# A two-layer graph attention kernel: fewer rows of a node summed on TensorE in layer 1, and another order of loads at the seam between the layers

## The chip, the cores and the metric

The kernel runs on one core of one Trainium2 chip. The metric is the device time of one execution in microseconds (us). Before the change, three timed executions took 5579.89, 5581.57 and 5582.52 us; the median, 5581.57 us, is the time before. A further execution was recorded by the hardware profiler and took 5586.68 us.

The engines are named as the profile names them: PE is TensorE (PEld its weight loads), DVE is VectorE, ACT is ScalarE, POOL is GpSimd, and SP is the engine from whose queue most plain DMAs are issued. Each engine works through its own instructions in program order and waits on semaphores for the others.

## What is computed

The reference is a graph attention network of two layers with residual paths, on 10,000 nodes of 768 features and 170,000 edges (self loops included; the layers add one more self loop to each node). Cut to what matters:

```python
def gat_conv(x, edge_index, W, a_src, a_dst, bias, heads, out_ch, concat):
    ei = _add_self_loops(edge_index, n)
    src, dst = (ei[0], ei[1])
    xl = (x @ W).reshape(n, heads, out_ch)
    alpha_src = einsum('nhc,hc->nh', xl, a_src)
    alpha_dst = einsum('nhc,hc->nh', xl, a_dst)
    e = leaky_relu(alpha_src[src] + alpha_dst[dst], 0.2)
    e = exp(e - segment_max(e, dst)[dst])
    alpha = e / (segment_sum(e, dst)[dst] + 1e-16)
    out = segment_sum(xl[src] * alpha[:, :, None], dst)
    ...
h = relu(layer_norm(gat_conv(x, ..., W1, ..., 4, 256, True), g1, be1)) + (x @ Wr1 + br1)
h = layer_norm(gat_conv(h, ..., W2, ..., 1, 768, False), g2, be2) + (h @ Wr2 + br2)
x = layernorm(x + h)
```

Layer 1 has 4 heads of 256 columns (1024 together), layer 2 one head of 768. Everything is 32-bit floating point.

## The kernel before, in words

**Blocks.** Nodes are sorted by their number of incoming edges and cut into 79 blocks of 128, one node to a partition. A block t has SLOTS[t] slots: slot k holds, for each of the 128 nodes, the table row of its k-th neighbour. The program fixes the number of slots of each block in advance, 8 to 41, 1377 in all. The blocks are taken in an order in which the slots rise to 41 in the middle (block 39) and fall again. Below, n is the number of slots of a block. "Row" means one slot: one gathered row for each of 128 nodes. 

**Three stages.** Stage 0 multiplies x by W1 and writes table 1; beside it `prepare()` sorts the nodes on the other engines, and `weight_steps()` loads W2, adds two columns to it, loads Wr1, and computes the product of br1 with W2, whose results are the tile `lift` and the DRAM row `shift`. Then `ordered_layer1()` and `ordered_layer2()` run one after the other. (`general_path()` is for inputs that do not fit; it does not run here.)

**A block of layer 1.** POOL gathers rows of table 1 into a ring of 28 slots (`Ring.fetch`, L413), each with one indirect DMA of 128 rows. A slot is fetched again when its row was used. When all rows of the block are there, `logits` (L458 to L466) and `normalised` compute the attention weights e. The weighted sum is then split:

- the first m rows, m = `on_pe(t)`, are summed on PE: for each row and head ACT makes a diagonal matrix of the weights (L691) and PE multiplies it with the row into PSUM (L697). The rows 0 and 1 come first, then the rest in a second batch;
- of the other rows, `weigh` adds to the same PSUM tile on DVE. Counted from m, every fourth row is multiplied and added on DVE (four instructions at L496, one for each head); the three behind it are multiplied on ACT (L485, four instructions) and added on DVE with one instruction (L492).

The sums of block t+1 are prepared inside block t: `logits` is issued when block t has three rows left, the diagonals and PE sums behind it, if the two blocks fit into the ring. The statistics of the finished block (`deviation`, L538 to L542) and its normalisation (`scaled`, L551 to L554) follow on DVE. On ACT, the square root of the statistics (L542) stands between the two batches of diagonals. Behind the second batch stands `store(t - 2)`: ACT copies the finished row of an earlier block (L716), POOL scatters it into table 2 (L718), and behind that stand POOL's next gathers. PE further does transposes (L560), x times Wr1 (`product(xT, wr1, ...)`) and h times W2 (`product(hT, w2, ...)`), both at L166. `to_layer2` stores h for the second layer (L767, on SP's queue).

**The seam.** `ordered_layer2` gathers from table 2 into a ring of 38 slots. It loads Wr2 into the place of W2 (the tile w2), so this load follows the last product of layer 1; six pieces of the tile wr1 serve as buffers for h, x and a work tile. ACT's queue issues the loads of b2, g2, be2, br2, br1 and, behind an addition on DVE, `shift`. DVE adds br2 to be2 (L817), spreads br1 (L576), adds `shift` to b2 (L821), and only then comes to the logits of block 0.

**A block of layer 2.** PE computes x + h times Wr2 in PSUM (`residual`, L862 and L865); columns 0 to 511 of the attention sum are made on DVE (L496), columns 512 to 767 on PE with diagonals (L846, L851) into the residual's PSUM tile. `residual(t + 1)` is issued at the head of block t. In front of block 0 stands `residual(0)`, then the product of br1 with Wr2, then `residual(1)`, and only then the PE sums of block 0. A ring slot is free when both DVE and PE have used its row.

Of the kernel before, what the change touches and what calls it, by code (L numbers as in the profile page):

```python
# [34 lines left out]
P = 128  # L35
# [13 lines left out]
DIAGONALS = 5  # L49
ON_PE2 = 512  # L50
SHARE = 4
ON_PE1 = 5


def chunk_counts(n_edges):
# [23 lines left out]
def gnn_kernel(ctx, tc, x, x_cols, src, dst, src_col, dst_col, W1, a_src1, a_dst1, b1, g1, be1, Wr1, br1,  # L79
# [50 lines left out]
    loops = consts.tile([P, NT], F32, name="loops")  # L130
    fits = consts.tile([1, 1], I32, name="fits")
    lift = consts.tile([P, 1], F32, name="lift")

    def spread(pool, v, name):

        n = v.shape[-1] if len(v.shape) == 1 else v.shape[0] * v.shape[1]
        b = pool.tile([P, n], F32, name=name)
        nc.scalar.dma_start(b, bass.AP(tensor=v.tensor, offset=v.offset, ap=[[0, P], [1, n]]))
        return b

    def weights(pool, w, name, more=0):
# [17 lines left out]
    def product(aT, w, n, pool=None):  # L159

        k = w.shape[1]
        p = (pool or ps_big).tile([P, 2 * BANK], F32, name="big")
        for c in range(0, n, BANK):
            e = min(n, c + BANK)
            for j in range(k):
                nc.tensor.matmul(p[:, c:e], aT[:, j, :], w[:, j, c:e], start=(j == 0), stop=(j == k - 1))  # L166
        return p
# [399 lines left out]
    def load(s, w):  # L567
        nc.sync.dma_start(s[:, :, :w.shape[1]], w.rearrange("(k p) n -> p k n", p=P))

    def spread_br1(pool, name):  # L570

        b = pool.tile([P, K1], F32, name="br1_c")
        with nc.allow_non_contiguous_dma(reason="1024 numbers"):
            nc.scalar.dma_start(b, br1.rearrange("(k p) -> p k", p=P))
        to = pool.tile([P, K1, P], F32, name=name)
        nc.vector.tensor_copy(to, b[:, :, None].to_broadcast([P, K1, P]))  # L576
        return to

    wp = ctx.enter_context(tc.tile_pool(name="wp", bufs=1, side="right"))
# [2 lines left out]
    with tc.tile_pool(name="w1", bufs=1) as w1p, tc.tile_pool(name="l1", bufs=2) as io, \  # L582
            psum_for_products(), tc.manual_schedule():
        w1 = w1p.tile([P, K0, C1], F32, name="w1")
        xTs = {}

        def load_x(t):
            if t < NT:
                xTs[t] = io.tile([P, K0, P], F32, name="xT", bufs=3)
                nc.sync.dma_start(xTs[t], x_cols[t])  # L590

        load_x(0)
        for k in range(K0):
            nc.sync.dma_start(w1[:, k, :], W1[k * P:(k + 1) * P, :])
        load_x(1)
        as_b, ad_b = spread(w1p, a_src1, "as1_b"), spread(w1p, a_dst1, "ad1_b")
        none = w1p.tile([P, R1], F32, name="none")[:1]
        nc.vector.memset(none[:, :C1], 0.0)
        nc.vector.memset(none[:, C1:], -BIG)
        nc.scalar.dma_start(table1[NP:NP + 1, :], none)  # L600
        nc.scalar.dma_start(table2[NP:NP + 1, :], none[:, C1 - C2:C1 + 2 * H2])


        b1_b = w1p.tile([P, R1], F32, name="none")[:, :C1]
        nc.scalar.dma_start(b1_b, bass.AP(tensor=b1.tensor, offset=b1.offset, ap=[[0, P], [1, C1]]))

        def weight_steps():

            brT = spread_br1(w1p, "brT")
            yield
            yield
            load(w2, W2)
            for i, a in enumerate((a_src2, a_dst2)):
                vec = spread(w1p, a, "a2")
                for k in range(K1):
                    yield
                    m = io.tile([P, C1], F32, name="scr")[:, :C2]
                    nc.vector.tensor_mul(m, w2[:, k, :C2], vec)  # L620
                    nc.scalar.activation(m, m, AF.Copy, accum_out=w2[:, k, C2 + i:C2 + i + 1])
            load(wr1, Wr1)
            yield
            q = product(brT, w2, R2)
            row = io.tile([P, R1], F32, name="row")
            nc.scalar.copy(row[:, :R2], q[:, :R2])
            nc.vector.tensor_add(lift, row[:, C2:C2 + 1], row[:, C2 + 1:R2])
            nc.scalar.dma_start(shift, row[0:1, :C2])


        steps = itertools.zip_longest(prepare(), weight_steps())
        for t in range(NT):
            p = product(xTs.pop(t), w1, C1)
            row = io.tile([P, R1], F32, name="row")
            nc.scalar.copy(row[:, :C1], p[:, :C1])  # L635
            for i, vec in enumerate((as_b, ad_b)):
                m = io.tile([P, C1], F32, name="scr")
                nc.vector.tensor_mul(m, p[:, :C1], vec)  # L638
                for h in range(H1):
                    s = slice(h * DH1, (h + 1) * DH1)  # L640
                    nc.scalar.activation(m[:, s], m[:, s], AF.Copy,
                                         accum_out=row[:, C1 + i * H1 + h:C1 + i * H1 + h + 1])
            nc.gpsimd.tensor_add(row[:, :C1], row[:, :C1], b1_b)  # L643
            load_x(t + 2)
            nc.sync.dma_start(table1[t * P:(t + 1) * P, :], row)
            next(steps, None)
        for _ in steps:
            pass
# [7 lines left out]
    def ordered_layer1():  # L656
        nonlocal ps_big
        with tc.tile_pool(name="b1", bufs=1) as pool, tc.tile_pool(name="small1", bufs=2) as small, \
# [15 lines left out]
            def on_pe(t):  # L674


                return min(max((2 * SLOTS[t] - 15) // 5, 1), ON_PE1, SLOTS[t])

            def weights_of(t):

# [123 lines left out]
    def ordered_layer2():  # L804
        nonlocal ps_big
        with tc.tile_pool(name="b2", bufs=1) as pool, tc.tile_pool(name="small2", bufs=2) as small, \
                tc.tile_pool(name="ps_acc2", bufs=2, space=PSUM) as ps_acc, \
                tc.tile_pool(name="ps_q2", bufs=3, space=PSUM) as ps_big, tc.manual_schedule():
            ring = Ring(pool, table2, R2, RING2)
            ring.fetch(SLOTS[0])  # L810

            wr2, parts = w2[:, :, :C2], [wr1[:, k, :] for k in range(K0)]
            load(wr2, Wr2)
            b2_b, g2_b, be2_b = (spread(pool, v, n) for v, n in ((b2, "b2"), (g2, "g2"), (be2, "be2")))
            more = pool.tile([P, C2], F32, name="out")
            nc.scalar.dma_start(more, bass.AP(tensor=br2.tensor, offset=br2.offset, ap=[[0, P], [1, C2]]))
            nc.vector.tensor_add(be2_b, be2_b, more)  # L817
            brT = spread_br1(pool, "brT")
            more = pool.tile([P, C2], F32, name="out")
            nc.scalar.dma_start(more, shift.to_broadcast([P, C2]))  # L820
            nc.vector.tensor_add(b2_b, b2_b, more)  # L821

            def fetch_x(t):

# [64 lines left out]
            ins = {t: fetch_x(t) for t in range(min(2, NT))}  # L889
            ring.fetch(RING2)  # L890
            rs = {0: residual(0)}
            q = product(brT, wr2, C2)
            last = iter(())
            ready = []
            assert whole(0) and NT > 1
            for t in range(NT):
                n = SLOTS[t]
                if t + 1 < NT:
                    rs[t + 1] = residual(t + 1)
                h = parts[4 + t % 2][:, :C2]  # L900
                if not whole(t):
                    for _ in last:
                        pass
                    ad = small.tile([P, H2], F32, name="ad")
                    nc.vector.tensor_add(ad, ring.slot(FIRST[t])[:, C2 + H2:], lift)
                    attend_parts(small, ring, h, h, ad, b2_b, H2, DH2, t)
                    last = norms(t, h, rs[t], [h])
                else:
                    e = (ready or list(weights_of(t)))[0]
                    acc = ps_acc.tile([P, BANK], F32, name="acc")  # L910
                    next(last, None)
                    ready, ahead, turn = [], iter(()), n
                    if t + 1 < NT and SLOTS[t + 1] + LEAD <= ring.size:

                        ahead = weights_of(t + 1)
                        turn = min(max(n // 3, n + SLOTS[t + 1] + 2 * LEAD - ring.size), n - LEAD)
                    for k in range(n):
                        if k in (turn, turn + LEAD):
                            ready += itertools.islice(ahead, 1)
                        if k in (LEAD, 2 * LEAD, 3 * LEAD):  # L920
                            next(last, None)
                        weigh(acc, ring.slot(FIRST[t] + k), e[:, k], ON_PE2, None if k else b2_b)
                        ring.fetch(FIRST[t] + k + 1 + ring.size)
                        if t + 2 < NT and k == n // 2:
                            ins[t + 2] = fetch_x(t + 2)
                    ready += ahead
                    for _ in last:
                        pass
                    if not t:
                        nc.vector.tensor_add(be2_b, be2_b, q[:, :C2])  # L930
                    last = norms(t, h, rs[t], [acc, rs[t][:, C2:2 * C2 - ON_PE2]])
                if t + 2 < NT and t + 2 not in ins:
                    ins[t + 2] = fetch_x(t + 2)
# [272 lines left out]
```

## Time and profile before

| What | Before |
|---|---|
| profiled execution | 5586.68 us |
| its span, first to last instruction | 5584.8 us |
| PE busy | 4822.9 us (86%) |
| DVE busy | 4279.6 us (77%) |
| POOL busy | 3367.2 us (60%) |
| ACT busy | 3140.8 us (56%) |
| mean load of the DMA engines | 283 GB/s |
| granted TensorE clock, mean | 0.939 |
| stage 0 | 0 to 892 us (first gather of layer 1) |
| layer 1 | 892 to 3540 us (first gather of layer 2) |
| layer 2 | 3540 us to the end |

Read the busy shares stage by stage. In layer 1 (892 to 3540 us) PE is busy for 2285 of 2648 us, DVE for 2179, ACT for 2045, POOL for 1455. In layer 2 PE is busy for 1682 of 2045 us, DVE for 1616, POOL for 1490, ACT for 740. POOL's busy time is the time of its DMA instructions; between two of them lie about 0.30 us of issue that is not counted as busy.

The period of a block of layer 1, taken from one store of h (L767) to the next, is 25.1 us where one row is summed on PE, 26.9 with two, 28.6 with three at 15 and 16 slots, 29.7 at 17 slots, about 32 at 19 slots, 35 to 38 at 20 slots, and 47 to 52 at 24 to 27 slots.

### The profile page before, as it was taken

How to read it: one execution, taken by the hardware profiler on the slowest of the kernel's cores; microseconds unless marked ns; L12 is line 12 of the kernel's file. 1: busy time of each engine (PE TensorE's matmuls, PEld its weight loads, DVE VectorE, ACT ScalarE, POOL GpSimd, SP SyncE). 2: the span in 40 equal slices, each digit the busy share in tenths (PEclk: the TensorE clock that was granted, in tenths of full speed). 3: DMA queues.
4: the chain of work that ended last, by engine and by line, in shares of the span. 5: the costliest groups of instructions: out<-in, count | busy, mean ns of one | idle time of the engine just before them, and what ended most of it. 6: DMA issues, size and time to landing. Idle time of an engine off the chain costs nothing. (4 is left out here: it accounts for less than half of the span.)

```text
span 5584.8 us, 58282 instructions
## 1 busy us (share of the span) xinstructions
PE 4822.9 (86%) x15304; PEld 2875.9 (51%) x15304; DVE 4279.6 (77%) x7692; ACT 3140.8 (56%) x8177; POOL 3367.2 (60%) x3396
## 2 busy tenths in 40 slices
PE   9999997999998874678899999799988737888988
PEld 3444443555555542345555555466555525555555
DVE  5783344888988778777899888498877776778888
ACT  3433444788888776677888887243333312334333
POOL 2446465555655554455566553477777776777775
PEclk9999998999999997789999999899998878999999
DMA  4322426899998887788999986699999987999996
GB/s 156 123 93 81 100 90 258 304 324 334 338 348 331 312 306 289 276 306 323 339 356 346 343 319 238 244 339 340 332 332 330 331 290 261 332 327 328 336 335 235
DMA packets 438663, 1581.00 MB, mean 283 GB/s; under 512 B 102763, under 2 KB 106923, under 8 KB 438326
## 3 DMA queue, kind: packets, MB, share of 16 engines
q0 software_dynamic: 341344, 1400.80, 69.9%
q1 hardware_dynamic: 93168, 170.98, 9.1%
q10 hardware_dynamic: 3814, 5.39, 0.3%
q8 instruction: 129, 2.11, 0.1%
q14 instruction: 208, 1.70, 0.1%
HBM read 1431.10 MB, written 146.19 MB: 282 GB/s over the span
## 5 line engine op out<-in xcount | busy, mean ns | idle before, releaser
L413 POOL DMA_INDIRECT ring<-table,slots x2754 | 2626.3, 954 | 1361.8 <-issue 290.4
L496 DVE SCALAR_TENSOR_TENSOR acc<-ring,e,acc 128x256 f32<-128x256 f32 (+1 forms) x2486 | 1546.5, 622 | 193.0 <-PE acc L697 119.4
L485 ACT ACTIVATE ring<-ring,e 128x256 f32<-128x256 f32 x3236 | 1317.2, 505 | 0.0
L492 DVE TENSOR_TENSOR acc<-acc,ring 128x1024 f32<-128x1024 f32 x809 | 996.6, 1232 | 71.2 <-ACT ring L485 2.1
L865 PE MATMUL big<-w,wr 128*128 128x512 f32 (+1 forms) x2528 | 877.4, 501 | 0.0
L166 PE MATMUL big<-w,xT 128*128 128x512 f32 x1896 | 823.7, 596 | 19.8 <-DMA w<-in_W_dram 9.4
L166 PE MATMUL big<-w,hT 128*128 128x512 f32 (+1 forms) x2528 | 830.4, 486 | 1.2 <-ACT hT L563 1.2
L166 PE MATMUL big<-wr,xT 128*128 128x512 f32 x1896 | 830.4, 595 | 0.7 <-ACT xT L563 0.7
L851 PE MATMUL big<-ring,diagonals 128*128 128x256 f32 x2672 | 646.6, 403 | 153.0 <-ACT diagonals L850 121.5
L697 PE MATMUL acc<-ring,diagonals 128*128 128x256 f32 x2088 | 516.6, 407 | 265.9 <-ACT diagonals L691 265.8
L865 PEld LDWEIGHTS big<-w,wr 128*128 128x128 f32 x2528 | 494.4, 196 | 369.6 <-issue 335.8
L166 PEld LDWEIGHTS big<-w,hT 128*128 128x128 f32 x2528 | 478.3, 189 | 373.5 <-issue 340.7
L851 PEld LDWEIGHTS big<-ring,diagonals 128*128 128x128 f32 x2672 | 533.5, 202 | 262.5 <-ACT diagonals L850 168.1
L166 PEld LDWEIGHTS big<-w,xT 128*128 128x128 f32 x1896 | 361.8, 192 | 479.2 <-issue 460.7
L697 PEld LDWEIGHTS acc<-ring,diagonals 128*128 128x128 f32 x2088 | 424.4, 206 | 351.0 <-ACT diagonals L691 253.2
L166 PEld LDWEIGHTS big<-wr,xT 128*128 128x128 f32 x1896 | 356.1, 191 | 418.5 <-issue 417.4
L850 ACT ACTIVATE diagonals<-ident,e 128x128 f32<-128x128 f32 x1336 | 398.6, 387 | 152.8 <-DVE e L476 113.5
L542 ACT ACTIVATE sd<-mv,eps 128x1 f32<-128x1 f32 x237 | 69.8, 294 | 592.8 <-DVE mv L540 592.3
L638 DVE TENSOR_TENSOR scr<-big,as_b 128x1024 f32<-128x1024 f32 x79 | 96.7, 1225 | 382.0 <-ACT row L635 382.0
L691 ACT ACTIVATE diagonals<-ident,e 128x128 f32<-128x128 f32 x1044 | 318.9, 387 | 110.8 <-DVE e L476 110.8
L643 POOL TENSOR_TENSOR row<-row,none 128x1024 f32<-128x1024 f32 x79 | 186.9, 2366 | 270.4 <-ACT row L635 269.9
L466 ACT ACT_TABLE_LOAD x153 | 196.3, 1283 | 238.8 <-DVE e L465 210.2
(169 smaller groups left out, 3971.4 us busy)
## 6 DMA issues: line engine op xcount, KB each, us to landing
ring<-table,slots POOLq DMA_INDIRECT x2754, 6.0
table<-row SPq DMA_DIRECT2D x79, 516.0 KB, 2.9
h_d<-hT SPq DMA_DIRECT2D x79, 512.0 KB, 7.2
wr<-h_d SPq DMA_DIRECT2D x79, 512.0 KB, 6.9
xT<-in_x_cols_dram SPq DMA_DIRECT2D x79, 384.0 KB, 4.4
w<-in_W_dram SPq DMA_DIRECT2D x6, 512.0 KB, 7.3
w<-in_W_dram SPq DMA_DIRECT2D x1, 3072.0 KB, 13.4
wr<-in_Wr_dram SPq DMA_DIRECT2D x1, 3072.0 KB
```

The lines of the kernel that those rows point to most:

```text
L166: nc.tensor.matmul(p[:, c:e], aT[:, j, :], w[:, j, c:e], start=(j == 0), stop=(j == k - 1))
L413: nc.gpsimd.indirect_dma_start(out=to, out_offset=None, in_=table, in_offset=bass.IndirectOffsetOnAxis(ap=index, axis=0), **more)
L466: nc.scalar.activation(e, e, AF.Exp)
L485: nc.scalar.activation(row[:, s], row[:, s], AF.Copy, scale=e[:, h:h + 1])
L492: nc.vector.tensor_add(acc[:, :c], acc[:, :c], row[:, :c])
L496: nc.vector.scalar_tensor_tensor(acc[:, s], row[:, s], e[:, h:h + 1], (acc if first is None else first)[:, s], op0=OP.mult, op1=OP.add)
L643: nc.gpsimd.tensor_add(row[:, :C1], row[:, :C1], b1_b)
L691: nc.scalar.activation(diagonals[:, k * H1 + i, :], ident, AF.Copy, scale=e[:, k, i:i + 1])
L697: nc.tensor.matmul(acc[:, c:d], diagonals[:, k * H1 + i, :], ring.slot(FIRST[t] + k)[:, c:d], start=(k == 0 and c % BANK == 0), stop=(k == ...
L850: nc.scalar.activation(diagonals[:, k % G, :], ident, AF.Copy, scale=e[:, k, :])
L851: nc.tensor.matmul(to, diagonals[:, k % G, :], ring.slot(FIRST[t] + k)[:, ON_PE2:C2], start=False, stop=(k == n - 1), skip_group_check=True)
L865: nc.tensor.matmul(r[:, c:d], hT[:, j, :], wr2[:, j, c:d], start=False, stop=(j == K1 - 1 and (d < C2 or not whole(t))), skip_group_check= ...
```

## The change

Three edits go together.

1. `on_pe(t)` changes from (2n - 15)/5 with at most 5 to n/2 - 5 with at most 4 (both rounded down, at least 1). Of the 79 blocks, the 5 with n = 13 go from two rows to one, the 8 with n = 15 from three to two, and the 21 with n = 20 to 27 from five to four; the others keep their number (block 39 with n = 41 does not fit into the ring and makes no PE sums). The tile of the diagonals shrinks from 20 to 16 matrices.
2. At the seam Wr2 is loaded into the tile wr1 and the buffers move to the tile w2. The loads of b2, g2, be2, br2 and `shift` move from ACT's queue to SP's, in front of the gathers in the program and behind the load of Wr2. br1 is loaded once, in stage 0, into a tile that stays.
3. The product of br1 with Wr2 and `residual(1)` are issued behind the PE sums of block 0, no longer in front of them.

```diff
-ON_PE1 = 5
+ON_PE1 = 4
...
+    br1_c = consts.tile([P, K1], F32, name="br1_c")
+
+    def spread(pool, v, name, queue=None):
...
-        nc.scalar.dma_start(b, bass.AP(tensor=v.tensor, offset=v.offset, ap=[[0, P], [1, n]]))
+        (queue or nc.scalar).dma_start(b, bass.AP(tensor=v.tensor, offset=v.offset, ap=[[0, P], [1, n]]))
...
     def spread_br1(pool, name):
...
-        b = pool.tile([P, K1], F32, name="br1_c")
-        with nc.allow_non_contiguous_dma(reason="1024 numbers"):
-            nc.scalar.dma_start(b, br1.rearrange("(k p) -> p k", p=P))
         to = pool.tile([P, K1, P], F32, name=name)
-        nc.vector.tensor_copy(to, b[:, :, None].to_broadcast([P, K1, P]))
+        nc.vector.tensor_copy(to, br1_c[:, :, None].to_broadcast([P, K1, P]))
         return to
...
-            brT = spread_br1(w1p, "brT")
+            with nc.allow_non_contiguous_dma(reason="1024 numbers"):
+                nc.scalar.dma_start(br1_c, br1.rearrange("(k p) -> p k", p=P))
             yield
             yield
+            brT = spread_br1(w1p, "brT")
             load(w2, W2)
...
-                return min(max((2 * SLOTS[t] - 15) // 5, 1), ON_PE1, SLOTS[t])
+                return min(max(SLOTS[t] // 2 - 5, 1), ON_PE1, SLOTS[t])
...
+            wr2 = wr1.rearrange("p k n -> p (k n)")[:, :K1 * C2].rearrange("p (k n) -> p k n", n=C2)
+            load(wr2, Wr2)
+            parts = pieces(w2.rearrange("p k n -> p (k n)")[:, :6 * C1], C1)
+            b2_b, g2_b, be2_b = (spread(pool, v, n, nc.sync)
+                                 for v, n in ((b2, "b2"), (g2, "g2"), (be2, "be2")))
+            adds = [spread(pool, br2, "out", nc.sync), spread(pool, shift, "brT", nc.sync)]
             ring = Ring(pool, table2, R2, RING2)
             ring.fetch(SLOTS[0])
-
-            wr2, parts = w2[:, :, :C2], [wr1[:, k, :] for k in range(K0)]
-            load(wr2, Wr2)
-            b2_b, g2_b, be2_b = (spread(pool, v, n) for v, n in ((b2, "b2"), (g2, "g2"), (be2, "be2")))
-            more = pool.tile([P, C2], F32, name="out")
-            nc.scalar.dma_start(more, bass.AP(tensor=br2.tensor, offset=br2.offset, ap=[[0, P], [1, C2]]))
-            nc.vector.tensor_add(be2_b, be2_b, more)
+            nc.vector.tensor_add(be2_b, be2_b, adds[0])
+            nc.vector.tensor_add(b2_b, b2_b, adds[1][:, :C2])
             brT = spread_br1(pool, "brT")
-            more = pool.tile([P, C2], F32, name="out")
-            nc.scalar.dma_start(more, shift.to_broadcast([P, C2]))
-            nc.vector.tensor_add(b2_b, b2_b, more)
...
             rs = {0: residual(0)}
-            q = product(brT, wr2, C2)
...
-                if t + 1 < NT:
+                if 0 < t < NT - 1:
                     rs[t + 1] = residual(t + 1)
...
                     acc = ps_acc.tile([P, BANK], F32, name="acc")
+                    if not t:
+                        q = product(brT, wr2, C2)
+                        rs[1] = residual(1)
                     next(last, None)
```

In the changed program's own order of instructions, SP issues the load of Wr2 in front of the last store of h, waiting only for the last product of x with Wr1. The other four constants and `shift` follow the last store of h and wait for the buffers of layer 1; the first two loads of h (L826 before) stand behind them. POOL's order is the same as before, instruction by instruction.

More of the change, by code (lines that the diff above doesn't have):

```diff
@@ L132, in gnn_kernel @@
     lift = consts.tile([P, 1], F32, name="lift")
-    def spread(pool, v, name):
+    br1_c = consts.tile([P, K1], F32, name="br1_c")
+    def spread(pool, v, name, queue=None):
         n = v.shape[-1] if len(v.shape) == 1 else v.shape[0] * v.shape[1]
         b = pool.tile([P, n], F32, name=name)
-        nc.scalar.dma_start(b, bass.AP(tensor=v.tensor, offset=v.offset, ap=[[0, P], [1, n]]))
+        (queue or nc.scalar).dma_start(b, bass.AP(tensor=v.tensor, offset=v.offset, ap=[[0, P], [1, n]]))
         return b
```

## The prediction, made before the changed kernel ran

> **What bounds the kernel now.** I read the table of windows first, stage by stage, then the periods of single blocks, then the timeline inside a block, then the seam. Stage 0 is PE work without gaps and only a copy on DVE moves in it. Layer 1 has two regimes. This is the windows table (columns: window, length; busy us and instructions of PE, PEld, DVE, ACT, POOL; granted clock, DMA share, GB/s):
>
> ```profile
> 1100.00:1300.00 200.00, 192.96 (x652) 114.92 (x651) 172.12 (x269) 166.40 (x401) 113.59 (x119) 1.00 0.91 322
> 1800.00:2100.00 300.00, 249.56 (x816) 155.47 (x815) 229.89 (x344) 229.84 (x577) 165.43 (x176) 0.93 0.85 315
> 3100.00:3300.00 200.00, 192.96 (x652) 114.92 (x651) 176.35 (x278) 166.43 (x401) 116.21 (x123) 1.00 0.93 336
> 3600.00:4400.00 800.00, 714.64 (x2452) 475.06 (x2451) 663.51 (x1396) 319.48 (x776) 607.73 (x632) 0.94 0.94 333
> ```
>
> In the flanks (first and third line) PE is busy 96% at full clock: PE is the limit. In the middle (second line) no engine is above 83%: something there waits in a ring. In layer 2 (fourth line) POOL issues 632 instructions in 800 us, one each 1.27 us, without a pause longer than its issue time: POOL's queue is the limit, PE close behind.
>
> The middle, block 30 (n = 20, five rows on PE), from the timelines of its engines, and below the dots block 26 (n = 19, four rows):
>
> ```profile
> 1783.26 10.59 PE L697 MATMUL acc<-ring,diagonals 128*128 128x256 f32 x40 [2.87 <-ACT diagonals L691]
> 1786.93 3.60 ACT L691 ACTIVATE diagonals<-ident,e 128x128 f32<-128x128 f32 x12
> 1790.44 0.78 ACT L716 COPY row<-big 128x770 f32<-128x770 f32 x1
> 1791.50 1.01 POOL L718 DMA_INDIRECT table<-row,order  x1 [3.44 <-ACT row L716]
> 1792.81 0.97 POOL L413 DMA_INDIRECT ring<-table,slots  x1 [0.30 <-PE acc L697]
> 1793.89 2.06 DVE L496 SCALAR_TENSOR_TENSOR acc<-ring,e,acc 128x256 f32<-128x256 f32 x4 [3.08 <-PE acc L697]
> ...
> 1649.17 2.43 ACT L691 ACTIVATE diagonals<-ident,e 128x128 f32<-128x128 f32 x8
> 1652.56 1.01 POOL L718 DMA_INDIRECT table<-row,order  x1 [2.27 <-ACT row L716]
> 1653.36 2.06 DVE L496 SCALAR_TENSOR_TENSOR acc<-ring,e,acc 128x256 f32<-128x256 f32 x4 [0.32 <-PE acc L697]
> ```
>
> The ring holds 28 slots, two blocks of 20 need 40. So 12 gathers of the next block must follow rows of this one, and they stand on POOL behind the scatter L718, that behind the copy L716, that behind the second batch of diagonals. Then they run off one each 1.25 us, and the next logits follow 23 us after the first (1792.8 to 1815.5): the DMA of 12 rows. With n = 19 it is 10 gathers and 20 us (1653.9 to 1673.9), so 1.5 us a row. The period is thus a chain: weights, diagonals, copy, scatter, gathers. Beside it DVE waits 3.08 us for the PE sums with five rows, 0.32 us with four.
>
> **Part 1, the rows.** A PE row is 8 matmul records; 16 of them took 3.62 us in the flank, so 1.81 us with its start, and the period rises by 1.72 us a row (25.13, 26.86, 28.58). 34 rows go.
>
> *Flanks.* A row on DVE is 1.30 us when ACT multiplied it (1.23 and a gap), 2.1 us when every fourth (four times 0.5). n = 15 goes from 12 rows on DVE (3 fourth, 9 shared) to 13 (4, 9): +2.1 us. PE would allow 26.86. But 17 slots with three on PE (14 rows: 4, 10) has period 29.78 with DVE waiting nowhere; minus one shared row that is 28.48, and 16 slots (13 rows) indeed waits 0.1 to 0.2 us at 28.58. So n = 15 becomes 28.4: -0.2 each, -1.2 us over 8 blocks. n = 13 goes from 11 to 12 DVE rows; n = 14 with 12 rows waits 0.5 us for PE at 26.86, so DVE allows 26.4 and PE 25.13: -0.45 each, -2.2 us over 5. Flanks together **-3.4 us**: PE's gain is nearly all taken by DVE.
>
> *Middle.* For the 21 blocks with n = 20 to 27 the second batch falls from 12 diagonals to 8: 3.60 against 2.43 us, so copy, scatter and first gather are 1.2 us earlier. Slots 0 to 3 are free by then (PE starts 2.3 us after the exponential; two rows take 4 to 5 us). Row 4 moves to DVE, +1.3 us (16 blocks) or +2.1 us (n = 21, 25), but DVE starts about 2.8 us earlier, because its wait for PE falls from 3.08 to about 0.3. So every later row is used no later than before, and the DMA chain starts 1.2 us earlier: 21 x 1.2 = **-25 us**. The fourth-row pattern shifts by one: for n = 21, 25 one dearer row moves in front of the statistics (+0.65 us, five blocks), for n = 23, 27 it leaves (three blocks): +1 us; and for n = 20 and 24 it leaves the place beside the exponential: -0.3 us each for eight. I count these as zero. Bounds of the middle: 0 if the gathers wait for something else; -3.08 + 1.3 = -1.8 us a block, -38 us, if DVE's progress counts and not only the scatter; above zero see rival D.
>
> A rule that speaks against it: the Trainium skill, "TensorE: Matmul & The Clock Gate", section "HAM oscillation — how this bites in real kernels", says that idle gaps of PE over about 3.4 us throttle the clock. The row: block 30 waits 2.87 us and its 40 records then take 10.59 us, 0.26 each against 0.226 at full clock, so the start is partly slow already; block 26 waits 1.68 us and is not slow (3.72 us for 16). Less PE work lengthens the gap in the middle by about 2.0 - 1.2 = 0.8 us a block. By the rule the six blocks of n = 20, with gaps around 3 us, could lose up to 1.7 us each (half of 3.4; an estimate from the page), 10 us. By the rows this lies on the PE sums, whose end then is at most 1 us behind DVE's readiness, and not on the diagonals, the copy and the scatter. I take the rows: 0, and keep +6 us for the range.
>
> **Part 2, the seam.**
>
> ```profile
> 3574.57 0.96 DVE L821 TENSOR_TENSOR b<-b,out 128x768 f32<-128x768 f32 x1 [1.96 <-DMA out<-shift]
> ...
> 3592.16 0.94 POOL L413 DMA_INDIRECT ring<-table,slots  x1 [0.30 <-issue]
> 3599.37 0.94 POOL L413 DMA_INDIRECT ring<-table,slots  x1 [6.26 <-PE big L851]
> ```
>
> The first line: DVE reaches the logits of block 0 only at 3575.6, behind the late load of `shift`. The others are POOL's timeline: its one stop after the seam, 6.26 us, ring full, until PE sums block 0 (from 3598.4) behind `residual(0)` (3561.7 to 3575.7), the br1 product (10.5 us) and `residual(1)` (11.7 us). POOL is the limit of layer 2, so this stop is worth its length.
>
> - Wr2 (3 MB, issued 3530.5) is now issued when the last x product ends, about 3506, where the DMA engines idle (0 GB/s from 3505 to 3515). On SP the last h store stands behind it, and not late: its data come at 3519.9. The load leaves the first gathers alone: before, they got almost no bytes until 3545. Also four pauses of POOL between 3557 and 3579 (about 2.6 us together), while the engines were full, go.
> - Constants on SP: 5 issues of 0.4 us, at about 3539.3 as on ACT before, since they wait for layer 1's buffers. Behind them the two loads of h slip from 3531.0 to about 3541.5. Moved until block 0's x lands: 9 gathers 3.5 MB, constants 2.0, h 1.0; at 0.39 MB per us (3560 to 3570) 17 us, about 3558 against 3561.7. So `residual(0)` runs 3558 to 3571, block 0's sums end at 3576, the br1 product at 3586, `residual(1)` at 3598, block 1's sums begin at 3598.5.
> - POOL reaches slot 38 at 3540 + 40 x 1.25 = 3590.5, finds block 0's 8 slots free, and with one gather of x comes to block 1's at 3602: no stop. That is 6.26 + 2.6 = 8.9 us earlier. PE reaches `residual(2)` at 3604 against 3610.5, 6.5 us earlier. I take -7.5 us. Bounds: -10, and 0 if the h loads are late by more than 7 us.
> - br1 in stage 0: DVE's 2.1 us wait at 28.5 goes, where DVE is idle anyway: 0. The later br1 load (4-byte pieces) goes: 0, inside the seam.
>
> **Sum**: -3.4 - 25 - 7.5 = **-36 us**. The profiled execution would go from 5586.7 to 5550.8; the median of the timed runs lies 5.1 us lower, so the forecast is 5581.6 - 36 = **5546 us**.
>
> **Rivals.**
> - B: the scatter is not what starts the chain (POOL waits for slots or data in any case). For it: 38.0 us of POOL's waits in the middle (1800 to 2100) are for DVE L492, against 22.9 for L716. Against: those lie behind a full ring, and the gathers behind L718 start at once after it. Then only flanks and seam count: -11, 5571.
> - C: DVE's start counts, and shorter blocks also help the next: -1.8 x 21 = -38, with -3.4 and -10: -51, 5530. For it: the period falls from 36.5 (n = 20) to 32.4 (n = 19), 4 us for one slot, of which 2 are bytes.
> - D, slower: DVE becomes the bound of layer 1. The middle adds 16 x 1.3 + 5 x 2.1 = 31 us to DVE. If PE still kept it waiting as long as now (the clock rule at work), the next logits would wait for DVE's rows: +31, with -7.5 from the seam and 0 from the flanks: +24, 5605. It decides once DVE's start moves up by less than 1.5 us. Against: the 0.32 us at block 26, and that DVE waits for gathers before nearly each middle logits (299.0 us in all, DVE L458).
> - E: the h loads and constants hold up block 0 by 10 us: seam +3, sum -25, 5556.
>
> **How the numbers follow.** A 0.56, B 0.13, C 0.17, D 0.09, E 0.05. A's own range is 5533 to 5558. For 8 in 10 I need B and C too and leave out most of D: 5522 to 5572. About 0.2%, 11 us, is what can be told from no change. Faster by more: A, C, E and 4 parts of B: 0.82. Within: the rest of B and a bit of D: 0.09. Slower: 0.09.
>
> **What would show it.** In the changed profile: no PE period of layer 1 above 28.6 us at n = 15; at n = 20 the wait of DVE L496 for PE about 0.3 us and the wait of POOL L718 for L716 about 2.3 us, the period near 35.4; POOL without a stop of more than 1 us between 40 and 100 us after the first layer-2 gather; L697 at 1816 records. Wrong would be a DVE wait for PE that stays at 3 us, a logits wait that vanishes in the middle, or a first `residual` later than 22 us after the first layer-2 gather.

## The result and the profile after

| | Before | After |
|---|---|---|
| timed runs, median | 5582.05 us (4 runs, 5579.89 to 5584.10) | 5547.6 us (4 runs, 5542.35 to 5550.57) |
| ratio after to before, 95% interval | | 0.9937 [0.992, 0.9955] |
| span of the profiled execution | 5584.8 us | 5540.6 us |
| left flank, blocks 0 to 20 | 557.95 us | 551.94 us |
| middle, blocks 20 to 53 | 1327.00 us | 1303.58 us |
| right flank, blocks 53 to 77 | 673.22 us | 669.86 us |
| last scatter of layer 1 to first gather of layer 2 | 8.35 us | 3.97 us |
| first 100 gathers of layer 2 | 152.30 us | 148.57 us |

The ratio is worth -35 us. The profile of after was its quickest execution, so the two spans differ by 44 us. The sections in the lower half are measured in the traces, from one store of h to the next. They have a spread of their own: in the six profiles with five rows in the middle (before, e1, e3, e6, e7, e8) it took 1321.7 to 1327.0 us. The profile of before stands at the upper end of that, so a good part of its 23 us there is spread. The sizes below come from timed runs where there are any.

**Middle, block 30.** These are the timelines of four engines of the changed kernel, put one under the other (start, length, engine, line; in brackets the idle time before it and what ended it):

```profile
1772.01 3.72 PE L697 MATMUL acc<-ring,diagonals 128*128 128x256 f32 x16 [2.62 <-ACT diagonals L691]
1776.12 3.72 PE L697 MATMUL acc<-ring,diagonals 128*128 128x256 f32 x16 [0.39 <-ACT diagonals L691]
...
1775.68 2.43 ACT L691 ACTIVATE diagonals<-ident,e 128x128 f32<-128x128 f32 x8
1778.02 0.78 ACT L716 COPY row<-big 128x770 f32<-128x770 f32 x1
...
1779.08 1.01 POOL L718 DMA_INDIRECT table<-row,order  x1 [2.27 <-ACT row L716]
1780.39 0.96 POOL L414 DMA_INDIRECT ring<-table,slots  x1 [0.30 <-issue]
...
1779.88 2.06 DVE L497 SCALAR_TENSOR_TENSOR acc<-ring,e,acc 128x256 f32<-128x256 f32 x4 [0.32 <-PE acc L697]
```

Read it from the second batch of diagonals: 2.43 us where it was 3.60, then the copy, the scatter, the first gather. The scatter waits 2.27 us for the copy where it waited 3.44. This block also shows the DVE wait at 0.32 us, but it is a favourable one. Over the whole execution the page gives DVE's four-instruction rows and the PE sums like this (busy us, mean ns of one, idle before and the part of its main releaser), and below the dots the same two groups in the kernel before:

```profile
L497 DVE SCALAR_TENSOR_TENSOR acc<-ring,e,acc 128x256 f32<-128x256 f32 (+1 forms) x2538 | 1572.1, 619 | 127.9 <-PE acc L697 52.4
L697 PE MATMUL acc<-ring,diagonals 128*128 128x256 f32 x1816 | 459.6, 412 | 273.4 <-ACT diagonals L691 240.9
...
L496 DVE SCALAR_TENSOR_TENSOR acc<-ring,e,acc 128x256 f32<-128x256 f32 (+1 forms) x2486 | 1546.5, 622 | 193.0 <-PE acc L697 119.4
L697 PE MATMUL acc<-ring,diagonals 128*128 128x256 f32 x2088 | 516.6, 407 | 265.9 <-ACT diagonals L691 265.8
```

52.4 us of waiting for PE stay, of 119.4. Taken block by block over 19 middle blocks (29 to 37 and 41 to 50), the wait is 1.44 us on average, after 3.04. PE has 272 records fewer, but its mean record is longer, 412 ns after 407, and it idles a little longer before the sums, 273.4 us after 265.9. The windows table (columns as in the prediction: window, length, five engines, clock, DMA share, GB/s):

```profile
1100.00:1300.00 200.00, 191.23 (x627) 111.11 (x626) 181.84 (x288) 163.87 (x389) 115.48 (x121) 0.99 0.92 328
1800.00:2100.00 300.00, 227.38 (x730) 141.14 (x730) 238.49 (x361) 220.74 (x545) 162.84 (x173) 0.87 0.86 317
3600.00:4400.00 800.00, 710.55 (x2433) 474.84 (x2433) 654.69 (x1361) 315.25 (x769) 606.82 (x631) 0.93 0.94 334
```

In the window from 1800 to 2100 us the granted clock is 0.87, before 0.93. Over the whole middle, 1600 to 2750 us, the difference is small: 0.89, before 0.90. In the flank DVE is busy for 181.84 of 200 us, before 172.12. Layer 2, after its start, is what it was.

**The seam**, POOL's timeline with PE's below the dots:

```profile
3498.13 0.97 POOL L718 DMA_INDIRECT table<-row,order  x1 [12.88 <-ACT row L716]
3502.10 0.98 POOL L414 DMA_INDIRECT ring<-table,slots  x1 [3.00 <-DMA table<-row,order]
3519.64 0.94 POOL L414 DMA_INDIRECT ring<-table,slots  x1 [1.01 <-DMA ring<-table,slots]
3521.68 0.94 POOL L414 DMA_INDIRECT ring<-table,slots  x1 [1.10 <-DMA ring<-table,slots]
3524.03 0.94 POOL L414 DMA_INDIRECT ring<-table,slots  x1 [1.41 <-DMA ring<-table,slots]
3600.48 0.94 POOL L414 DMA_INDIRECT ring<-table,slots  x1 [0.86 <-DVE acc L497]
...
3524.84 2.05 PE L861 MATMUL big<-w,ident 128*128 128x512 f32 x2 [27.87 <-DMA w<-in_x_dram,order]
3539.37 3.72 PE L850 MATMUL big<-ring,diagonals 128*128 128x256 f32 x16
3542.93 10.48 PE L167 MATMUL big<-wr,brT 128*128 128x512 f32 x32
```

The same two lines of POOL in the kernel before:

```profile
3531.67 0.97 POOL L718 DMA_INDIRECT table<-row,order  x1 [12.88 <-ACT row L716]
3540.01 0.98 POOL L413 DMA_INDIRECT ring<-table,slots  x1 [7.38 <-DMA table<-row,order]
```

Layer 2's gathers wait until the last scatter has landed: 7.38 us before, 3.00 now. The PE sums of block 0 (L850) stand in front of the br1 product (L167), 37 us after the first gather, and the ring is not full for POOL: its longest stop between 40 and 100 us after the first gather is 0.86 us. But it pauses three times at 3519 to 3524 us for earlier gathers to land.

### The profile page after: what moved, and what is told of

Its sections match the earlier page's. It is cut to its first block, busy times and chain, and to the rows that moved or that the text cites. A ratio compares the mean times of both kernels' runs of the same rounds, so it can differ in the third digit from the quotient of the medians.

```text
span 5540.6 us, 57764 instructions
## 1 busy us (share of the span) xinstructions
PE 4768.5 (86%) x15032; PEld 2830.2 (51%) x15032; DVE 4328.0 (78%) x7765; ACT 3133.9 (57%) x8125; POOL 3369.6 (61%) x3396
## 5 line engine op out<-in xcount | busy, mean ns | idle before, releaser
L497 DVE SCALAR_TENSOR_TENSOR acc<-ring,e,acc 128x256 f32<-128x256 f32 (+1 forms) x2538 | 1572.1, 619 | 127.9 <-PE acc L697 52.4
L486 ACT ACTIVATE ring<-ring,e 128x256 f32<-128x256 f32 x3320 | 1350.9, 506 | 0.0
L493 DVE TENSOR_TENSOR acc<-acc,ring 128x1024 f32<-128x1024 f32 x830 | 1022.5, 1232 | 72.3 <-ACT ring L486 0.9
L864 PE MATMUL big<-wr,w 128*128 128x512 f32 (+1 forms) x2528 | 870.3, 498 | 0.0
L167 PE MATMUL big<-w,xT 128*128 128x512 f32 x1896 | 822.2, 595 | 21.9 <-DMA w<-in_W_dram 11.2
L167 PE MATMUL big<-wr,xT 128*128 128x512 f32 x1896 | 835.9, 597 | 0.7 <-ACT xT L564 0.7
L167 PE MATMUL big<-w,hT 128*128 128x512 f32 (+1 forms) x2528 | 830.4, 486 | 1.2 <-ACT hT L564 1.2
L850 PE MATMUL big<-ring,diagonals 128*128 128x256 f32 x2672 | 654.7, 407 | 152.0 <-ACT diagonals L849 135.2
L697 PE MATMUL acc<-ring,diagonals 128*128 128x256 f32 x1816 | 459.6, 412 | 273.4 <-ACT diagonals L691 240.9
L864 PEld LDWEIGHTS big<-wr,w 128*128 128x128 f32 x2528 | 493.5, 195 | 362.0 <-issue 329.4
L850 PEld LDWEIGHTS big<-ring,diagonals 128*128 128x128 f32 x2672 | 539.0, 204 | 264.3 <-ACT diagonals L849 167.9
L167 PEld LDWEIGHTS big<-w,hT 128*128 128x128 f32 x2528 | 477.7, 189 | 374.0 <-issue 339.9
L167 PEld LDWEIGHTS big<-w,xT 128*128 128x128 f32 x1896 | 360.7, 191 | 480.3 <-issue 461.2
L167 PEld LDWEIGHTS big<-wr,xT 128*128 128x128 f32 x1896 | 357.8, 192 | 422.3 <-issue 421.3
L697 PEld LDWEIGHTS acc<-ring,diagonals 128*128 128x128 f32 x1816 | 373.2, 208 | 352.8 <-ACT diagonals L691 262.0
L849 ACT ACTIVATE diagonals<-ident,e 128x128 f32<-128x128 f32 x1336 | 398.7, 387 | 148.9 <-DVE e L477 115.0
L691 ACT ACTIVATE diagonals<-ident,e 128x128 f32<-128x128 f32 x908 | 278.5, 387 | 109.7 <-DVE e L477 109.7
```

Of the source, the lines that this page charges most:

```text
L486: nc.scalar.activation(row[:, s], row[:, s], AF.Copy, scale=e[:, h:h + 1])
L493: nc.vector.tensor_add(acc[:, :c], acc[:, :c], row[:, :c])
L497: nc.vector.scalar_tensor_tensor(acc[:, s], row[:, s], e[:, h:h + 1], (acc if first is None else first)[:, s], op0=OP.mult, op1=OP.add)
L691: nc.scalar.activation(diagonals[:, k * H1 + i, :], ident, AF.Copy, scale=e[:, k, i:i + 1])
L697: nc.tensor.matmul(acc[:, c:d], diagonals[:, k * H1 + i, :], ring.slot(FIRST[t] + k)[:, c:d], start=(k == 0 and c % BANK == 0), stop=(k == ...
L849: nc.scalar.activation(diagonals[:, k % G, :], ident, AF.Copy, scale=e[:, k, :])
```

## The experiments

Ratios are to the kernel before, each with the runs of the same session beside it; times in microseconds are the ratio's distance from 1 times 5582.

**The three parts, each alone.** e1 is the changed kernel with the old rows:

```diff
-ON_PE1 = 4
+ON_PE1 = 5
...
-                return min(max(SLOTS[t] // 2 - 5, 1), ON_PE1, SLOTS[t])
+                return min(max((2 * SLOTS[t] - 15) // 5, 1), ON_PE1, SLOTS[t])
```

> The changed kernel with the old number of PE rows: the seam alone. Theory: layer 1 as before; the last scatter lands 4 us after its issue and no longer 8 (Wr2 is loaded already), so layer 2 begins 4.4 us earlier, and POOL's stop of 6.3 us goes: -10.7 us, 5571. Rival, the seam as I predicted it (stop and pauses only, no earlier start): -7.5, 5574. If the profile of the changed kernel owed its seam gain to other luck: between 0 and -4.

e2 is the kernel before with at most four rows, which only touches the 21 blocks of the middle:

```diff
-                return min(max((2 * SLOTS[t] - 15) // 5, 1), ON_PE1, SLOTS[t])
+                return min(max((2 * SLOTS[t] - 15) // 5, 1), 4, SLOTS[t])
```

> The kernel before, with at most four rows on PE, all else as before: only the 21 blocks of 20 to 27 slots change. Theory (the scatter starts the chain, 4 diagonals fewer stand in front of it, 1.2 us a block): -25 us, 5557. Rival C (DVE's earlier start counts): -38. Rival B: 0. Rival D (DVE becomes the bound): +31.

e3 is the kernel before with the new rows in the blocks of 13 and 15 slots only:

```diff
-                return min(max((2 * SLOTS[t] - 15) // 5, 1), ON_PE1, SLOTS[t])
+                return min(max((2 * SLOTS[t] - 15) // 5 if SLOTS[t] > 19 else SLOTS[t] // 2 - 5, 1), ON_PE1, SLOTS[t])
```

> The kernel before, with the new number of rows for blocks up to 19 slots (13: one, 15: two) and five for the large ones. My prediction's step (DVE takes nearly all back): -3.4 us. The profile of the changed kernel shows -9.5 in these stretches: full PE periods of 25.1 and 26.9 us at the first blocks, until DVE's lead is used up. If that is the cause and not a side effect of the middle: -8 to -10, 5573.

| | ratio, interval | us | the prediction's term |
|---|---|---|---|
| e1, seam | 0.9989 [0.998, 0.9998] | -6 (-11 to -1) | -7.5 |
| e2, middle rows | 0.9969 [0.9958, 0.9981] | -17 (-23 to -11) | -25 |
| e3, flank rows | 0.9984 [0.9975, 0.9993] | -9 (-14 to -4) | -3.4 |
| sum | | -32 | -36 |
| all three | 0.9937 [0.992, 0.9955] | -35 (-45 to -25) | -36 |

The parts add up to the whole within their intervals. Two of the three terms, the middle's and the flanks', lie just outside theirs, in opposite directions. The interval of e1 holds both the -10.7 us expected for it and the prediction's -7.5; the runs do not tell the two apart.

**e4: is it the scatter or DVE's start?** The changed kernel with four diagonals more in the second batch of the large blocks. Nobody reads them; ACT takes the time it took with five rows, PE and DVE have the work of four:

```diff
+                    if lo and n > 19:
+                        for i in range(H1):
+                            nc.scalar.activation(diagonals[:, m * H1 + i, :], ident, AF.Copy,
+                                                 scale=e[:, m, i:i + 1])
```

> The changed kernel, but in blocks of over 19 slots ACT makes four further diagonals in the second batch that nobody reads, so that the scatter comes as late as with five rows, while PE and DVE work as in the changed kernel. If the 1.2 us of the copy and scatter are the gain of the middle: the middle's -25 goes, the time rises to about 5572. If DVE's earlier start is the gain (rival C): it stays near 5548. The output is the same.

Measured: 0.9972 [0.996, 0.9983], -16 us: what seam and flanks give without the middle (-6 and -9). Block 30 of e4, from its timelines:

```profile
1778.19 2.43 ACT L691 ACTIVATE diagonals<-ident,e 128x128 f32<-128x128 f32 x8
1780.53 1.26 ACT L695 ACTIVATE diagonals<-ident,e 128x128 f32<-128x128 f32 x4
...
1782.75 1.01 POOL L722 DMA_INDIRECT table<-row,order  x1 [3.44 <-ACT row L720]
...
1783.42 1.54 DVE L497 SCALAR_TENSOR_TENSOR acc<-ring,e,acc 128x256 f32<-128x256 f32 x3 [1.36 <-PE acc L701]
```

The four added diagonals take 1.26 us, and the scatter's wait is back at 3.44 us, the value of before to the hundredth. DVE waits for PE 1.36 us only, as in a kernel with four rows. Means over the 19 middle blocks, from the traces, counted from the exponential of a block's weights:

| | to the first gather | from it to the next logits | to DVE's first row | DVE's wait for PE |
|---|---|---|---|---|
| before | 12.05 | 27.35 | 13.11 | 3.04 |
| e1 | 12.05 | 27.27 | 13.02 | 2.99 |
| after | 10.96 | 27.49 | 11.56 | 1.44 |
| e2 | 10.95 | 27.21 | 11.35 | 1.28 |
| e4 | 12.09 | 27.38 | 11.61 | 1.50 |
| e5 | 9.74 | 27.65 | 11.45 | 1.36 |

e4 separates the two: DVE begins its rows 1.5 us earlier than before, the first gather does not, and the middle (1323.68 us) is that of five rows. So what DVE gains there buys nothing. But e4 also gives ACT its old amount of work back, so it cannot by itself tell the early scatter from the lighter ACT. The next run can: it leaves ACT's work as it is and changes only the order.

**e5: more of the same.** If that chain sets the period, its scatter can go earlier still. The changed kernel with `store(t - 2)` in front of the second batch of diagonals:

```diff
+                if full is not None and n > 19:
+                    store(t - 2)
```

> The changed kernel, but in blocks of over 19 slots the copy of the finished row and its scatter stand in front of the second batch of diagonals. Theory (scatter and first gather start the chain): both come 2.4 us earlier in 21 blocks; the six of 20 slots come near the rate of the DMA engines and give 1.5 each, the others 2: -39 us, about 5509. Rival C (what counts is when DVE starts): the second batch is 0.8 us later, so +17, 5565. A further rival, the slots of rows 2 and 3 are freed too late by PE: a gain below 15 us.

Measured: 5528.7 us, 0.9907 [0.989, 0.9923], -52 us against before and -19 against the changed kernel (medians). It is the best version of this study. Its block 30:

```profile
1779.16 0.78 ACT L716 COPY row<-big 128x770 f32<-128x770 f32 x1
1779.84 2.44 ACT L691 ACTIVATE diagonals<-ident,e 128x128 f32<-128x128 f32 x8
...
1779.34 0.95 POOL L414 DMA_INDIRECT xt<-in_x_dram,order  x1 [0.31 <-PE acc L697]
1780.59 1.99 POOL L718 DMA_INDIRECT table<-row,order  x1 [0.30 <-ACT diagonals L691]
1782.89 0.97 POOL L414 DMA_INDIRECT ring<-table,slots  x1 [0.30 <-PE acc L697]
```

The copy now lies in front of the diagonals, about 2.3 us earlier (5.8 us behind the exponential instead of 8.1), but the first gather comes only 1.22 us earlier in the mean (10.96 to 9.74). The scatter no longer waits for the copy: it starts 0.30 us behind the gather of x that precedes it on POOL, which costs 0.4 us of the copy's gain in the mean of the 19 blocks. It also takes 1.99 us where it took 1.01, in the mean 1.73. The two together are half of the copy's gain, and the time gained is about half of what was expected: the middle went from 1303.58 to 1283.96 us in the traces, 0.9 us for each of the 21 blocks. ACT's work is that of the changed kernel, so the order alone gave this, and a lighter ACT is not needed to explain it.

Why the scatter takes longer can be read from DVE's timeline at the same place:

```profile
1780.42 1.28 DVE L555 SCALAR_TENSOR_TENSOR h<-h,sd,be 128x1024 f32<-128x1024 f32 x1
```

This instruction, the second half of the normalisation, takes both of its large inputs from SBUF. It was running when the scatter began, and the scatter ended 0.88 us after it. That is no accident of block 30: 44 of POOL's DMA instructions in e5 began while this instruction, of one block or another, had more than 0.2 us to run, and every one of them ended 0.81 to 0.89 us after it. In the changed kernel's block 30 the same instruction (1776.94 to 1778.23 us) was over before the scatter began. So the next limit in e5 is DVE's normalisation as well as the queue of POOL; no run has moved one of the two.

**e6 and e7: the seam in two parts.** e6 is the kernel before with Wr2 in the place of wr1, so that its load is issued early, and nothing else:

```diff
-            wr2, parts = w2[:, :, :C2], [wr1[:, k, :] for k in range(K0)]
+            wr2 = wr1.rearrange("p k n -> p (k n)")[:, :K1 * C2].rearrange("p (k n) -> p k n", n=C2)
+            parts = pieces(w2.rearrange("p k n -> p (k n)")[:, :6 * C1], C1)
```

> The kernel before, with Wr2 in the tile wr1 and the buffers in w2, nothing else. Theory: this alone shortens the way from the last scatter to the first gather of layer 2 from 8.35 us to about 4.0; POOL's stop of 6.3 us stays or grows, since gathers start earlier and PE's order is the old one. If the early constants caused it: 8.35 stays.

e7 is the kernel before with the product of br1 and `residual(1)` behind the sums of block 0, and nothing else:

```diff
-            q = product(brT, wr2, C2)
...
-                if t + 1 < NT:
+                if 0 < t < NT - 1:
                     rs[t + 1] = residual(t + 1)
...
+                    if not t:
+                        q = product(brT, wr2, C2)
+                        rs[1] = residual(1)
```

> The kernel before, with the br1 product and the second residual behind the PE sums of block 0, nothing else. Theory: POOL's stop of 6.3 us goes or falls below 2, the first 100 gathers of layer 2 take about 148 instead of 152 us, scatter to gather stays at 8.35. If the stop needs the early constants too (DVE comes to block 0 at 36 us after the first gather): it stays above 4.

Each was executed once, so they are read from their traces. POOL in e6:

```profile
3530.08 0.98 POOL L413 DMA_INDIRECT ring<-table,slots  x1 [3.00 <-DMA table<-row,order]
...
3588.99 0.94 POOL L413 DMA_INDIRECT ring<-table,slots  x1 [6.89 <-PE big L852]
```

and in e7:

```profile
3537.16 0.98 POOL L413 DMA_INDIRECT ring<-table,slots  x1 [7.31 <-DMA table<-row,order]
...
3605.56 0.94 POOL L413 DMA_INDIRECT ring<-table,slots  x1 [3.55 <-DVE sd L878]
...
3622.30 0.94 POOL L413 DMA_INDIRECT ring<-table,slots  x1 [1.93 <-PE big L851]
```

e6 has the short wait for the scatter and keeps the long stop. e7 keeps the long wait, and its stop is only cut up: 3.55 us, and 1.93 us some 15 us later; its first 100 gathers took 152.50 us, before 152.30. So the new place of Wr2 alone gives the 4.4 us at the scatter, the order alone gives nothing, and the stop goes only when Wr2, the constants and the order have all moved. The first of these holds beyond the single executions: in the five traces with Wr2 in its new place the scatter is followed by the first gather after 3.97 to 3.98 us, in the other five after 8.21 to 8.48. The first two loads of h move with Wr2, though (issued at 3521.94 us in e6, at 3530.98 right behind Wr2 before), so e6 does not say which of the two loads delayed the scatter. Which of the constants or Wr2 the order needs beside it was not tried.

**e8: the blocks of 13 slots alone**, on the kernel before, executed once:

```diff
-                return min(max((2 * SLOTS[t] - 15) // 5, 1), ON_PE1, SLOTS[t])
+                return 1 if SLOTS[t] == 13 else min(max((2 * SLOTS[t] - 15) // 5, 1), ON_PE1, SLOTS[t])
```

> The kernel before, with one PE row instead of two in the five blocks of 13 slots, nothing else. The step of my prediction (DVE allows 26.4 us): -0.45 a block, -2.2 in the two flanks together. The profile of the changed kernel reads as 25.1 us a block until DVE's lead is used up: -3.4 on the left, about -2 on the right, -5.5 together, with the 15-slot blocks the rest of -9.5.

In the traces the left flank took 554.99 us and the right 671.78, so -3.0 and -1.4 against before; e3, which also has the 15-slot blocks, took 551.65 and 669.65. So of its -9.9 us in the traces the five blocks of 13 slots make 4.4, the eight of 15 slots 5.5.

## Why the prediction held, and which terms were off

The forecast of 5546 us met 5547.6, and rival A, the chain over the scatter, is the one that the experiments support. That the number was met within 2 us is luck in part: the middle gave less than predicted and the flanks more, and the two errors cancel.

- **Middle: mechanism right, size too large.** Predicted: 21 blocks by 1.2 us, -25. Measured: -17 alone (e2, timed), about -20 between e4 and after in their traces. (In e2's trace, its quickest execution, the middle took 1299.57 us, 22 to 27 below the six with five rows; the timed runs decide.) The first gather came 1.09 us earlier in the mean, not 1.2, and the way from it to the next logits took 0.14 us longer. B (the scatter is not the start) would have left e2 at zero, and C (DVE's start counts) would have left a gain in e4's middle; both fall.
- **DVE's wait for PE: wrong, at no cost.** Predicted: from 3.08 to about 0.3 us. The mean is 1.44; 0.3 came out in block 30, 2.2 in block 31. The step that failed is the one that let PE end its sums when the diagonals allow, as it does in block 30. This is PE's line of block 31, to be read beside the two of block 30 above:

```profile
1807.06 9.71 PE L697 MATMUL acc<-ring,diagonals 128*128 128x256 f32 x32 [3.82 <-ACT diagonals L691]
```

PE idled 3.82 us before these 32 records, the granted clock over them was 0.73, and they took 9.71 us; in block 30 it idled 2.62 us, the clock was 1.00, and 16 records took 3.72. Over the 19 blocks the first 16 records took 5.86 us in the mean (5.60 before) and the clock during the sums was 0.77 (0.83 before), so the sums end 1.5 us earlier than before and not 2.8. This is the behaviour that the Trainium skill ("TensorE: Matmul & The Clock Gate", section "HAM oscillation — how this bites in real kernels") warns of. The length of the gap does not decide it alone here: in e2, block 31's sums took 8.80 us after a gap of 2.25 us, while block 32's ran at the full clock after 3.68. The prediction priced it at 0 because it lies on the sums and not on the scatter. e4 supports that: its sums end as early as those of the changed kernel, 1.5 us earlier than before, and its middle (1323.68 us) gains nothing from it.
- **D, DVE as the bound: did not come.** DVE has one row more in each of the 21 blocks, and still e5 took another 19 us from these blocks with DVE's work unchanged. The margin was thin by the prediction's own measure: D was to decide if DVE's start moved up by less than 1.5 us, and it moved by 1.55. Three rows on PE instead of four, which would give DVE one more, were not tried.
- **Flanks: too small by more than half.** Predicted -3.4, measured -9 (e3). The working took the settled pace of the blocks whose rows change. That pace was right: from one exponential to the next, the steps to blocks 12, 13 and 14 take 28.25 to 28.40 us (predicted 28.4), those among the 13-slot blocks of the right flank 26.0 to 26.5 (predicted 26.4). It left out the neighbours. Here are the exponentials of blocks 5 to 9 in the kernel before:

```profile
1028.37 0.25 ACT L466 ACTIVATE e<-e 128x52 f32<-128x52 f32 x1
...
1082.09 0.25 ACT L466 ACTIVATE e<-e 128x56 f32<-128x56 f32 x1
1110.53 0.25 ACT L466 ACTIVATE e<-e 128x56 f32<-128x56 f32 x1
1137.58 0.25 ACT L466 ACTIVATE e<-e 128x56 f32<-128x56 f32 x1
```

and in the changed kernel:

```profile
1028.13 0.25 ACT L467 ACTIVATE e<-e 128x52 f32<-128x52 f32 x1
...
1081.09 0.25 ACT L467 ACTIVATE e<-e 128x56 f32<-128x56 f32 x1
1107.14 0.25 ACT L467 ACTIVATE e<-e 128x56 f32<-128x56 f32 x1
1133.86 0.25 ACT L467 ACTIVATE e<-e 128x56 f32<-128x56 f32 x1
```

128x52 is 13 slots times 4 heads, 128x56 is 14 slots, which keep their two rows. From the first line to the next (two steps) it is 53.72 us before and 52.96 after; the step behind it, 1082 to 1110, falls from 28.44 to 26.05 us. That is 2.4 us on a step that belongs to 14-slot blocks. The traces hold more of it: in blocks 15 to 18, with 16 and 17 slots, the four steps shrank by 1.9 us together. That DVE enters them with less of a backlog is how I read this; no run tested it by itself. On the right the steps to the four 15-slot blocks are even about 1.0 us longer together, so the flanks' sum is a balance of gains and losses at the borders between row counts.

- **Seam: total about right, wrong make-up.** Predicted -7.5 as a stop of 6.26 us and four pauses of 2.6 us together that go, limited by PE's 6.5. In the trace the stop went. The pauses did not (of those read from the kernel before, only two, at 3557 and 3561 us, are idle time; the others are gathers that took 1.30 to 1.45 us): over the first 100 gathers POOL's idle time above its usual 0.30 us fell from 7.81 to 4.07 us, and without the stop's 5.96 it rose from 1.85 to 4.07. The DMA instructions that took over 1 us cost the same in both, 3.4 us above 0.95 us each. That leaves -3.7. Another -4.4, so that the traces show -8.1 in all, is the last scatter landing earlier (8.35 to 3.97 us), which the prediction had in front of it ("before, they got almost no bytes until 3545") and did not count; e6 shows that moving Wr2, and the loads of h with it, does it.
- **The signs named beforehand.** 1816 records, the scatter's wait of 2.3 us, periods of 35.07, 35.05 and 36.57 us at the three blocks of 20 slots ahead of the middle (35.4 was named) and POOL without a stop came as said. One warning sign was tripped: the first `residual` began 22.7 us after the first layer-2 gather, where later than 22 was to mean that the forecast is wrong (18 was worked out). The working took 0.39 MB per us for the loads in front of it; in this stretch, 3502 to 3526 us, the engines moved 289 to 362 GB/s. It did no harm, since the sums of block 0 now follow it directly and ended 41 us after the first gather, while POOL comes to the end of the ring of 38 slots only about 53 us after it.

## What to carry to other kernels

Where a ring of buffers couples engines, find the one instruction that the next refill stands behind, and follow its queue backwards over every engine: here 1.2 us of diagonals on ACT, with ACT 75% busy, was worth more than anything that PE or DVE gained. When that wait goes, look at what the instruction meets next, on its own queue and on other engines: in e5 a gather in front of the scatter and a DVE instruction beside it took half of the next gain. And when work moves between engines in a run of unequal blocks, cost the blocks next to the changed ones too, not only the settled pace of the changed ones.

## What the runs showed of the hardware that was not expected

- What waits for a small indirect scatter came 8.35 us after the scatter's start instead of 3.97 when a load of 3 MB and two of 0.5 MB were issued up to 1.1 us ahead of it (before against after). From 3535 to 3540 us of before the DMA engines were busy for a share of 1.00, from 3498 to 3502 us of after for 0.25. That the engines share their time between the loads and the scatter is the likely cause, not one that a run isolates.
- POOL's gathers pause for earlier gathers to land, 0.4 to 1.8 us at a time, about 15 to 22 us after the burst of layer 2 begins, in all ten traces. The big load is not needed for it: even in before it had landed at 3542.16 us, 14 us ahead of the first pause.
- An indirect DMA instruction on POOL took longer when it began while DVE was in the middle of `h<-h,sd,be` (L554 before, L555 after), whose two large inputs lie in SBUF. In each of the ten traces all that did so with more than 0.2 us of it left (27 to 44 a trace) ended 0.81 to 0.89 us after it; the scatter of e5's block 30 took 1.99 us this way, where it takes 1.01 otherwise. Beside `h<-h,big`, which has one of its inputs in PSUM, nothing of the kind is seen: the scatter of block 30 in the changed kernel began 0.48 us before the end of that instruction and took 1.01 us. This is read from the traces; no run moved the DVE instruction to test it.
